# Quantizing the first feed-forward's input in parts of 704 and 320 columns, with all scale arithmetic on VectorE

## Chip, cores and metric

The program runs on one core of one Trainium2 chip, as one launch. The metric is device microseconds of that core, as the median of several executions. The kernel before has three: 3436.64, 3437.43 and 3438.43 us, with a median of 3437.43 us.

A core has five engines that work side by side, each on its own instructions in order: TensorE (PE: matmuls, with its weight loads listed apart as PEld), VectorE (DVE), ScalarE (ACT), GpSimd (POOL) and SyncE (SP, which here only issues transfers). They meet through semaphores. SBUF and PSUM are the on-chip memories, and PSUM holds what matmuls write; this stage uses eight PSUM tiles of one bank each (4, 3 and 1 in three pools).

## What is computed

The reference has two layers on an input of 8 sequences of 512 tokens with 256 channels. The change lies in the first layer:

```python
x = L0_attn_x                                   # (8, 512, 256)
xn = _layernorm(x)
x = x + _L0_attn_ref(xn, ...) + _L0_ffn_ref(xn, w_gate, w_up, w_down)
```

`_L0_attn_ref` is a selective state-space model. It projects `xn` to 512 channels, runs a causal convolution of four taps, and from the result makes a step size `delta`, and vectors `B` and `C` of 16 states. For each channel and state it runs the recurrence `h = exp(delta*A)*h + delta*u*B` over the 512 tokens, and sums `h*C` over the states.

`_L0_ffn_ref` is a gated feed-forward with 704 inner channels, and every operand of its three products is first rounded to four bits and back, block by block:

```python
def fp4_quant_dequant(x):                       # blocks of 16 along the last axis
    scale = max(max|block| / 6, 1e-12)
    q = round_to_grid(|block / scale|) * sign * scale
gate, y = fp4(xn) @ fp4(w_gate).T, fp4(xn) @ fp4(w_up).T
out = fp4(silu(gate) * y) @ fp4(w_down).T
```

The second layer is a block-sparse attention beside two layers of windowed attention with a gated feed-forward. The change does not touch it.

## The kernel before

**Two stages.** The first layer is one stage and the second layer another. In the first stage each engine gets its instructions in exactly the order in which the Python program issues them (class `Ordered`, L42). So the program order decides what stands behind what on each engine. The second stage starts when the first one's memory comes free, and is ordered by a planner.

**The main loop (L748).** A sequence ("batch" b, 8 of them) has 4 chunks of 128 channels, and a chunk has 16 states, taken two at a time. So a batch has 32 groups, and g counts 256 groups over the whole stage. Where a group's place in its batch matters, this text writes o = g - 32b. In each pass the loop issues, for its group: on ACT the decays of group g+1 (`da`), on PE the sum of an earlier group's states (`sum_states(g-2)`, tile `y`), on DVE the first scan of group g, on PE the spreading of B for group g+1 (`bu`), on POOL `times_c(g-1)` (tile `hh`, 128x1024), then one call of `step()`, on DVE the second scan of g, and on DVE `product(g+1)` (two instructions on tile `bu`). Because PE takes its instructions in order, `bu` of group g+1 stands behind `y` of group g-2, and that needs `times_c(g-2)` on POOL.

**Strands and steps.** All other work of the stage runs as generators, called strands here: `head(b)` makes norm, projection, convolution, step sizes and B and C of a batch; `ffn(b)` is the feed-forward; `output(b)` is the last projection; `z` is a gate branch; `fp4_weights` quantizes the weights. Each call of `step()` (L730) goes once through the active strands in the order in which they were started, and moves each by one step if PSUM allows:

```python
def step():
    for s, (peak, kept) in list(active.items()):
        if held[0] + peak <= MM:              # MM = 4 PSUM banks
            held[0] += kept
            active[s] = next(s, None)
```

A strand that needs more banks than are left stays where it is until a later step. `skewed(units, stages, every)` (L169) runs units through a list of stages, one stage to a step, and starts a unit every `every` steps; a tuple such as `(turn, 0, 1)` says how many banks a stage frees and takes. From L721 on, strands are started at fixed groups: `head(b+1)` at o = -5, `ffn(b)` at o = -1 (18 and 6 for b = 0 and 1), `output(b-1)` at o = 4.

**The gate at a batch's end.** Two groups before a batch begins, its first channel chunk must be ready, and if it is not, the loop calls further steps until it is, with no group's work between them:

```python
while g + 2 < total and at(g + 2)[:2] not in ready:
    step()
```

These are called extra steps below. A chunk is ready when `deltas(0)` of its head has been issued (L505). The head's stages between are `rank` (a matmul into one bank), `parts`, `second` (another bank), `third`, `fifth`, `logs`, `sums`, `deltas`; `third` and `fifth` each free a bank.

**The feed-forward strand (L524).** It first quantizes `xn` in place, then waits until the batch before has left its products (`busy`), transposes `xn` into `xqt` (two units, three steps), and then sends four tiles of 128 tokens, one every five steps, through 20 stages: five for gate and up products (in one bank), five to quantize the 128x704 result `h`, three to transpose it (`turn`, one bank), two for the down product (one bank), which `add` puts onto `x`. The text numbers the steps of this tile pipeline s0 to s29.

**Quantizing (L184).** `fp4_stages(p, f)` gives the stages for a tile of f columns, so n = f/16 blocks. Where n/4 is odd, one stage `inverses` does three things on DVE: the blocks' largest magnitude, the scale, and its reciprocal. Largest magnitudes and reciprocals lie there in rows of four used out of five places. Where n/4 is even, this is three stages: `scales` (DVE: largest magnitude), `scale` (POOL: scale, a 128x32 instruction) and `invert` (DVE: reciprocal). Then follow in both cases `divide` (POOL), `magnitude` (ACT), `levels` (DVE, two instructions) and `multiply` (POOL, two instructions). Before, `h` and `w_down` with 704 columns (n/4 = 11) go the first way; `xn` in two halves of 512 columns, and the gate and up weights, go the second (n/4 = 8).

Of the kernel before, what the change touches and what calls it, by code (L numbers as in the profile page):

```python
# [17 lines left out]
P = 128  # L18
NB, L, D = 8, 512, 256
NT = L // P  # L20
# [3 lines left out]
FI = 704  # L24
# [31 lines left out]
def tile_kernel(ctx: ExitStack, tc: tile.TileContext, a: dict, out: bass.AP):  # L56
# [57 lines left out]
    with ExitStack() as s0:  # L114
# [54 lines left out]
        def skewed(units, stages, every):  # L169


            made = {}
            stages = [s if isinstance(s, tuple) else (s, 0, 0) for s in stages]
            for step in range((len(units) - 1) * every + len(stages)):
                todo = [(i, stages[step - i * every]) for i in range(len(units)) if 0 <= step - i * every < len(stages)]
                peak = held = 0
                for _, (_, frees, takes) in todo:
                    held += takes - frees
                    peak = max(peak, held)
                yield peak, held  # L180
                for i, (f, _, _) in todo:
                    made[i] = f(units[i], made.get(i))

        def fp4_stages(p, f):  # L184

            n = f // QB

            def blocks(x):
                return x.rearrange("p (n b) -> p n b", b=QB)

            def spread(x):
                return x.unsqueeze(2).to_broadcast([p, n, QB])

            def inverses(_, x):


                amax = sm.tile([P, n // 4, 5], FP, tag="q_rows", name="q_rows")[:p, :, :4]
                sc = sm.tile([P, FI // QB], FP, tag="q_sc", bufs=4, name="q_sc")[:p, :n]
                r = sm.tile([P, n // 4, 5], FP, tag="q_ri", name="q_ri")[:p, :, :4]
                at = x.rearrange("p (a c b) -> p a c b", c=4, b=QB)  # L200
                dve.tensor_reduce(amax, at, AX.X, ALU.max, apply_absolute_value=True)
                dve.tensor_scalar(
                    sc.rearrange("p (a c) -> p a c", c=4), amax, 1.0 / 6.0, 1e-12, ALU.mult, ALU.max
                )
                dve.reciprocal(r, sc.rearrange("p (a c) -> p a c", c=4))
                return x, sc, r

            def scales(_, x):
                amax = sm.tile([P, FI // QB], FP, tag="q_amax", name="q_amax")[:p, :n]
                sc = sm.tile([P, FI // QB], FP, tag="q_sc", bufs=4, name="q_sc")[:p, :n]  # L210
                r = sm.tile([P, FI // QB], FP, tag="q_r", name="q_r")[:p, :n]
                dve.tensor_reduce(amax, blocks(x), AX.X, ALU.max, apply_absolute_value=True)
                return x, amax, sc, r

            def scale(_, st):
                x, amax, sc, r = st
                pool.tensor_scalar(sc, amax, 1.0 / 6.0, 1e-12, ALU.mult, ALU.max)
                return st

            def invert(_, st):  # L220
                x, amax, sc, r = st
                dve.reciprocal(r, sc)
                return x, sc, r

            def divide(_, st):
                x, sc, r = st
                v = q.tile([P, FI], FP, tag="q_v", bufs=3, name="q_v")[:p, :f]
                if len(r.shape) == 3:
                    quads = [y.rearrange("p (a c b) -> p a c b", c=4, b=QB) for y in (v, x)]
                    pool.tensor_tensor(*quads, r.unsqueeze(3).to_broadcast([p, *r.shape[1:], QB]), ALU.mult)  # L230
                else:
                    pool.tensor_tensor(blocks(v), blocks(x), spread(r), ALU.mult)
                return x, sc, v

            def magnitude(_, st):
                m = q.tile([P, FI], BF, tag="q_m", bufs=3, name="q_m")[:p, :f]
                act.activation(m, st[2], AF.Abs, scale=2.0**22)
                return *st, m

            def levels(_, st):  # L240

                x, sc, v, m = st
                dve.tensor_scalar(m, m, (1.0 + 2.0**-7) * 2.0**22, None, ALU.max)

                dve.scalar_tensor_tensor(v, v, 1.0 - 2.0**-23, m, ALU.mult, ALU.add)
                return st

            def multiply(_, st):
                x, sc, v, m = st
                pool.tensor_tensor(v, v, m, ALU.subtract)
                pool.tensor_tensor(blocks(x), blocks(v), spread(sc), ALU.mult)
                return x

            scaled = [inverses] if n // 4 % 2 else [scales, scale, invert]
            return [*scaled, divide, magnitude, levels, multiply]
# [265 lines left out]
        def ffn(b):  # L524

            x, xn = xs[b], made[b][0]

            def first(i, _):
                return xn[:, 2 * i : 2 * i + 2, :].rearrange("p t d -> p (t d)")

            scales, *stages = fp4_stages(P, 2 * D)
            yield from skewed(range(2), [lambda i, _: scales(i, first(i, _)), *stages], 3)
            yield 0, 0
            while b - 1 in busy:
                yield 0, 0
            busy.add(b)
            xqt = one.tile([P, KC, L], FP, tag="xqt", name="xqt")

            def turn_x(k, _):
                ps = pmm.tile([P, L], FP, tag="mm", name="ps_tr")  # L540
                for t in range(NT):
                    pe.transpose(ps[:, t * P : (t + 1) * P], xn[:, t, k * P : (k + 1) * P], ident)
                return ps

            def put_x(k, ps):
                act.copy(xqt[:, k, :], ps)

            yield from skewed(range(KC), [(turn_x, 0, 1), (put_x, 1, 0)], 1)
            n = FI // 2

            def product(t, w, cols):
                ps = pmm.tile([P, L], FP, tag="mm", name="ps_gu")
                for k in range(KC):
                    pe.matmul(
                        ps[:, :n], xqt[:, k, t * P : (t + 1) * P], w[:, k, cols],
                        start=(k == 0), stop=(k == KC - 1),
                    )
                return ps

            def gate_up(half):  # L560
                cols = slice(half * n, (half + 1) * n)

                def gate(t, h):
                    return h, product(t, w_g, cols)

                def up(t, st):
                    h, ps = st
                    act.activation(h[:, cols], ps[:, :n], AF.Silu)
                    if half and t == NT - 1:
                        busy.remove(b)  # L570
                    return h, product(t, w_u, cols)

                def both(t, st):
                    h, ps = st
                    dve.tensor_tensor(h[:, cols], h[:, cols], ps[:, :n], ALU.mult)
                    return h

                return gate, up, both

            def down(t, ht):  # L580
                ps = pmm.tile([P, L], FP, tag="mm", name="ps_d")
                for c in range(NI):
                    m = min(P, FI - c * P)
                    pe.matmul(
                        ps[:, :D], ht[:m, c, :], w_d[:m, c, :], start=(c == 0), stop=(c == NI - 1)
                    )
                return ps

            def add(t, ps):
                dve.tensor_tensor(x[:, t, :], x[:, t, :], ps[:, :D], ALU.add)  # L590

            def begin(t, _):
                return gate0(t, q.tile([P, FI], FP, tag="q_src", bufs=4, name="h"))

            (gate0, up0, both0), (gate1, up1, both1) = gate_up(0), gate_up(1)
            stages = [
                (begin, 0, 1), (up0, 1, 1), (lambda t, st: gate1(t, both0(t, st)), 1, 1), (up1, 1, 1), (both1, 1, 0),
                *fp4_stages(P, FI),
                *to_inner(lambda t: q.tile([P, NI, P], FP, tag="ht", name="ht")), (down, 0, 1), (add, 1, 0),
            ]  # L600
            yield from skewed(range(NT), stages, 5)
            done(b)
# [3 lines left out]
        def done(b):  # L606

            left[b] = left.get(b, 2) - 1
            if left[b] == 0:
                act.dma_start(x1_d[b], xs.pop(b))  # L610
# [840 lines left out]
```

## Time and profile before

One execution was also taken with the profiler.

| quantity | value |
|---|---|
| median of the runs | 3437.43 us |
| the profiled execution: its time / its span | 3434.61 us / 3432.7 us |
| first stage (start to the second stage's first matmul) | about 1409 us |
| last scan of the first stage ends | about 1378.9 us |
| busy over the span: PE, DVE, ACT, POOL | 91%, 70%, 51%, 46% |
| busy from 800 to 1000 us, of 200: PE, DVE, ACT, POOL | 176.9, 186.7, 147.7, 149.2 us |

The span goes from the first to the last instruction of the program; the execution's time is 1.9 us longer. In the list of groups, a line such as "DVE RECIPROCAL q_r<-q_sc 128x32 x16" names engine, operation, the written and the read tile, and how often it ran. In the first stage all instructions carry the line L50 of the recording helper, so they are told apart by tiles: `q_amax` and `q_rows` are the largest magnitudes (of the second and the first way), `q_sc` the scales, `q_r` and `q_ri` the reciprocals, `q_v` the divided values, `q_m` the magnitudes. A wait is put down to the instruction that released it.

### The profile page before, as it was taken

To read this page: it belongs to the slowest core of one execution; us is meant where nothing else is said; L and a number is where in the kernel's file an instruction comes from. 1 tells how busy PE (TensorE), PEld (TensorE's weight loads), DVE (VectorE), ACT (ScalarE), POOL (GpSimd) and SP (SyncE) were. 2 spreads that over 40 slices of the span, in tenths; PEclk is the share of its full clock that TensorE was granted. 3 is DMA by queue.
4 is the path that set the end of the run, shared out by engine and by line. 5 is a ranking of instruction groups with operands and counts; after the bars stand their busy time and mean duration, and the time that the engine had idled before them with its cause. 6 is when DMAs were issued, how large, how long until landed. Compare 5 with 4: busy or idle time off the path is not lost.

```text
span 3432.7 us, 41004 instructions
## 1 busy us (share of the span) xinstructions
PE 3125.9 (91%) x14082; PEld 1631.9 (48%) x14084; DVE 2420.1 (70%) x4792; ACT 1757.4 (51%) x3468; POOL 1584.3 (46%) x1141
## 2 busy tenths in 40 slices
PE   5768898889898988899999999999999999999998
PEld 2324454444444444455555455455445545545545
DVE  7979898989898999665466465566556456556544
ACT  5666777677776766244244244244334334433533
POOL 3786868787868687323133123123223223312312
PEclk7879999999999999899999999999999999999999
DMA  3323332323232323201101111111110100100100
GB/s 112 111 87 109 105 121 83 128 98 124 98 123 95 116 102 129 95 32 51 45 32 51 45 46 38 45 48 41 42 54 32 63 33 32 63 33 32 57 33 7
DMA packets 88856, 239.39 MB, mean 70 GB/s; under 512 B 9657, under 2 KB 42425, under 8 KB 88649
## 3 DMA queue, kind: packets, MB, share of 16 engines
q1 hardware_dynamic: 87496, 232.59, 19.6%
q10 hardware_dynamic: 1152, 4.19, 0.3%
q8 instruction: 112, 1.84, 0.2%
q14 instruction: 96, 0.78, 0.1%
HBM read 227.05 MB, written 9.70 MB: 69 GB/s over the span
## 4 chain that ended last, share of the span: by engine, by line
PE 59%; DVE 24%; POOL 7%; ACT 5%; issue 4%; DMA 1%; DVEq 0%; POOLq 0%; SPq 0%; ACTq 0%
PE ps_qkv L1105 10%; DVE hh L50 8%; PE ps_g L1284 5%; PE y L50 4%; PE ps_a L1284 4%; PE ps_wo L1248 3%; PE lo L1218 3%; DVE bu L50 3%; PE ps_y L1319 3%; PE ps_w L1302 3%; PE pt L1204 2%; POOL hh L50 2%; PE ps_ls L1157 2%; PE ps_gu L50 2%; DVE cv L50 2%
## 5 line engine op out<-in xcount | busy, mean ns | idle before, releaser
L50 POOL TENSOR_TENSOR hh<-hh,cb 128x1024 f32<-128x1024 f32 x256 | 604.0, 2361 | 297.7 <-DVE hh L50 129.6
L50 DVE TENSOR_TENSOR_SCAN hh<-da,bu 128x512 f32<-128x512 f32 x512 | 614.3, 1207 | 0.2 <-ACT da L50 0.2
L50 PE MATMUL y<-hh,ident 128*128 128x512 f32 x1024 | 520.1, 638 | 60.0 <-POOL hh L50 59.0
L50 ACT ACTIVATE da<-delta,a_neg 128x512 f32<-128x512 f32 x512 | 356.5, 718 | 326.1 <-DVE hh L50 317.5
L50 DVE TENSOR_TENSOR bu<-du,bu 128x512 f32<-128x512 f32 x512 | 325.5, 681 | 53.0 <-PE bu L50 51.9
L50 PEld LDWEIGHTS y<-hh,ident 128*128 128x128 f32 x1024 | 202.2, 204 | 291.9 <-issue 176.7
L50 ACT ACT_TABLE_LOAD x242 | 310.5, 1283 | 22.9 <-DVE x L50 9.6
L1195 POOL TENSOR_TENSOR pr<-pr,lrs 128x512 f32<-128x512 f32 (+1 forms) x256 | 234.7, 933 | 177.6 <-DVE lrs L1193 141.7
L1124 POOL TENSOR_TENSOR r<-r,r 128x512 f32<-128x512 f32 x128 | 162.9, 1272 | 288.9 <-DVE r L1122 243.5
L50 PE MATMUL bu<-bp,sel 128*128 128x512 bf16 x510 | 174.0, 393 | 125.3 <-DVE hh L50 124.4
L1176 ACT ACTIVATE pr<-ps_ls,nm 128x256 f32<-128x256 f32 (+1 forms) x512 | 221.5, 448 | 123.3 <-DVE nm L1170 120.2
L1120 DVE TENSOR_TENSOR r<-ps_qkv,tab 128x512 f32<-128x512 f32 x128 | 88.2, 689 | 201.6 <-ACT sq L1119 199.6
L1290 ACT ACTIVATE gl<-ps_g,b 128x512 f32<-128x512 f32 x96 | 65.9, 686 | 313.8 <-PE ps_g L1284 313.8
L1034 ACT ACTIVATE pt_e<-ps_st 128x512 f32<-128x512 f32 x320 | 166.6, 597 | 108.3 <-PE ps_st L1028 102.2
L873 POOL MEMSET sa<- 128x1 f32 x16 | 1.6, 98 | 449.9 <-DVE sf L1306 357.0
L1072 POOL TENSOR_TENSOR x1s<-x1s,bsum 128x256 f32<-128x256 f32 x32 | 23.1, 723 | 371.2 <-DVE x1s L1071 371.2
L1284 PE MATMUL ps_g<-hn,wf 128*128 128x512 f32 x384 | 189.6, 614 | 4.1 <-DVE hn L1273 2.6
L1291 DVE SCALAR_TENSOR_TENSOR ht<-ps_a,b,gl 128x512 f32<-128x512 f32 x80 | 60.1, 751 | 187.2 <-PE ps_a L1284 165.7
L1170 DVE CUSTOM_DVE_ANT_0 ps_ls<-ps_ls,mask 128x256 f32<-128x256 f32 (+1 forms) x512 | 184.3, 422 | 5.8 <-PE ps_ls L1157 4.9
L1105 PE MATMUL ps_qkv<-wqkv,sf 128*128 128x512 f32 x384 | 182.4, 607 | 0.0
L1105 PE MATMUL ps_qkv<-wqkv,s 128*128 128x512 f32 x384 | 181.4, 608 | 0.2 <-DVE r L1122 0.2
L1204 PE MATMUL pt<-ident,pr 128*128 128x128 f32 x896 | 132.1, 283 | 32.6 <-POOL pr L1195 28.1
(213 smaller groups left out, 6200.3 us busy)
## 6 DMA issues: line engine op xcount, KB each, us to landing
cb<-c_d SPq DMA_DIRECT2D x256, 512.0 KB, 3.6
wqkv<-in_wqkv SPq DMA_DIRECT2D x16, 1536.0 KB, 7.6
wf<-in_wf SPq DMA_DIRECT2D x16, 1408.0 KB, 11.4
wf<-in_wf SPq DMA_DIRECT2D x16, 768.0 KB, 4.3
tab<-tab SPq DMA_DIRECT2D x18, 512.0 KB, 3.5
wo<-in_wo SPq DMA_DIRECT2D x16, 512.0 KB, 3.9
x<-in_x SPq DMA_DIRECT2D x8, 512.0 KB, 4.9
x<-x ACTq DMA_DIRECT2D x8, 512.0 KB, 3.0
```

Of the source, the lines that this page charges most:

```text
L50: return self.tc.keep_in_program_order(getattr(self.engine, name)(*args, **kwargs))
L1034: act.activation(pt, banks[g], AF.Exp)
L1105: pe.matmul(ps, shifted(s, k, t * P, P), wqkv[:, k, i * IN : (i + 1) * IN], start=(k == 0), stop=(k == KC - 1),)
L1124: pool.tensor_tensor(r1[:, i], r1[:, i], r2, ALU.add)
L1170: last = dve.tensor_tensor_reduce(at, at, msk[:, 2 * P - nk :], -1.0, 3e38, ALU.add, ALU.min, nm[:, i : i + 1])
L1176: act.activation(pr[:, at], banks[r][:, at], AF.Exp, bias=nm[:, i : i + 1], scale=-1.0, accum_out=rs[:, i : i + 1],)
L1195: pool.tensor_tensor(ph, ph, rs.unsqueeze(2).to_broadcast([P, 2, nk]), ALU.mult)
L1204: pe.transpose(pt[:, j * P : (j + 1) * P], pr[:, j * P : (j + 1) * P], ident)
L1218: pe.matmul(o[r * LD : (r + 1) * LD, i * P : (i + 1) * P], lv[:, keys[j], h * LD : (h + 1) * LD], prts[r][:, (i * nkt + j) * P : (i * nkt ...
L1248: pe.matmul(ps, wo[:, c, m * P : (m + 1) * P], ot[:, c, :], start=(c == 0), stop=(c == IN // P - 1),)
L1284: pe.matmul(dst, wf1[:, k, off : off + P], hn[:, k, :], start=(k == 0), stop=(k == KC - 1))
L1302: pe.matmul(ps, wf2[:n, c, m * P : (m + 1) * P], ht[c][:n], start=(c == 0), stop=(c == NHC - 1),)
```

## The change

`xn`, which lies as 1024 columns in each partition (4 token tiles of 256 channels), is quantized as one part of 704 columns and one of 320, in place of two halves of 512. The numbers of blocks are 44 and 20, n/4 is 11 and 5, both odd. So both parts go the way of `inverses`: the largest magnitude, the scale and the reciprocal all come from DVE in one stage, in the rows of four of five, and the stages `scale` on POOL and `invert` on DVE fall away for `xn`. The list of stages shrinks from seven to five; the second part still starts three steps after the first. All blocks of 16 and their arithmetic stay the same. The weights keep their stages.

```diff
             x, xn = xs[b], made[b][0]
-            def first(i, _):
-                return xn[:, 2 * i : 2 * i + 2, :].rearrange("p t d -> p (t d)")
-
-            scales, *stages = fp4_stages(P, 2 * D)
-            yield from skewed(range(2), [lambda i, _: scales(i, first(i, _)), *stages], 3)
+            flat = xn.rearrange("p t d -> p (t d)")
+            parts = [(flat[:, :FI], fp4_stages(P, FI)), (flat[:, FI:], fp4_stages(P, NT * D - FI))]
+            stages = [lambda i, st, k=k: parts[i][1][k](i, st if k else parts[i][0]) for k in range(len(parts[0][1]))]
+            yield from skewed(range(2), stages, 3)
             yield 0, 0
             while b - 1 in busy:
```

## The prediction

> **What bounds the kernel now.** I read the page's busy shares by slice first: the first stage (the left 16 of 40 slices) is bound by VectorE, with GpSimd close behind.
>
> ```profile
> DVE  7979898989898999665466465566556456556544
> ...
> POOL 3786868787868687323133123123223223312312
> ```
>
> Then the tile view of the scales:
>
> ```profile
> L50 DVE TENSOR_SCALAR q_sc<-q_rows x34: 198/199/200, 196.8 to 1388.5; 128x44 f32<-128x44 f32 x34
> L50 DVE RECIPROCAL q_ri<-q_sc x34: 428/429/430, 197.1 to 1388.7; 128x44 f32<-128x44 f32 x34
> ...
> L50 POOL TENSOR_SCALAR q_sc<-q_amax x24: 314/333/649, 66.2 to 1263.0; 128x32 f32<-128x32 f32 x16, 88x32 f32<-88x32 f32 x8
> L50 DVE RECIPROCAL q_r<-q_sc x24: 317/345/353, 70.9 to 1264.1; 128x32 f32<-128x32 f32 x16, 88x32 f32<-88x32 f32 x8
> ...
>   POOL q_sc L50: 8.1, 3
> ```
>
> Three times, 8.1 us in all, VectorE stood still for a 0.33 us scale. The timelines of POOL and DVE around one of these (b = 5) say why:
>
> ```profile
> 918.91 2.36 POOL L50 TENSOR_TENSOR hh<-hh,cb 128x1024 f32<-128x1024 f32 x1
> 921.25 2.42 POOL L50 TENSOR_SCALAR xn<-x,ln_mv,ln_rs 128x256 f32<-128x256 f32 x2
> 923.74 0.33 POOL L50 TENSOR_SCALAR q_sc<-q_amax 128x32 f32<-128x32 f32 x1
> ```
>
> ```profile
> 920.05 0.52 DVE L50 TENSOR_TENSOR h<-h,ps_gu 128x352 f32<-128x352 f32 x1 [0.26 <-PE ps_gu L50]
> 924.10 0.35 DVE L50 RECIPROCAL q_r<-q_sc 128x32 f32<-128x32 f32 x1 [3.53 <-POOL q_sc L50]
> ```
>
> POOL was late by a whole queue: it ran without a gap from 889.55 to 952. The wait is a symptom of that queue. Last, DVE's busy time by stretch (columns: stretch, length, busy), o = -4 to 12 around the starts of batches 2 and 5:
>
> ```profile
> 384.30:480.60 96.30, 84.13 (x119) 0.93 0.27 93
> ...
> 885.80:974.50 88.70, 79.79 (x111) 0.92 0.28 95
> ```
>
> Batch 2's start idles 12.2 us, batch 5's 8.9 (3 and 6: 14.1 and 8.2; 4: 7.5). Before batches 2 and 3 the loop made extra steps, before 4 to 7 none.
>
> **What the skill says.** "VectorE: DVE Perf Modes", What auto-detection actually checks: a single-source op takes a two-port mode if its outermost sizes are even or equal; the rows of four of five with 11 or 5 quads are meant against that. "SBUF — State Buffer", Who interferes with whom: VectorE in a two-port mode, or with two SBUF inputs, and GpSimd block each other for a whole instruction. The trace agrees: `q_m` in place takes 277 to 2360 ns, while the 128x44 `q_sc` never leaves 198 to 200.
>
> **The instructions.** Before, a batch costs DVE 2 x (0.647 largest magnitude + 0.349 reciprocal) = 1.99 us (groups of 740 to 1240 us). After, the 704 part costs 0.865 + 0.199 + 0.428 = 1.49 (rows of `h`). No row has the 320 form: lines through the two measured widths give 0.43 + 0.27, and the 20-wide scale lies between 0 and 0.199; I take 0.17, so 0.87 (ends 0.68, its share by width, and 1.0). DVE: +0.37 a batch, +3.0 in eight (ends +1.4 and +4). POOL loses 2 x 0.327 = 0.65 a batch; its divides and multiplies, ACT's magnitudes and `levels` keep their columns, and lines through their 512 and 704 rows keep their sums. No transfer is added. New wait: `levels` of part 0 comes at step 3 behind ACT's magnitude and POOL's divide at step 1. Behind it on DVE stand the second scan and `product`; POOL's queue below puts divide's end before that point, so I charge nothing; uncovered it costs up to the old 3.5 us in four batches.
>
> **The moved order.** Quantizing takes 3 + 5 = 8 steps, before 3 + 7 = 10. So `ffn`'s tile pipeline starts two steps earlier, at o = 12 for 14, and meets `head` at another point for the four banks. I counted banks by hand. The count for before reproduces the trace: batch 4's third tile is one step late (its first half product of `h` in group 155, not 154), as `head` holds 3 banks at o = 24 and the pipeline's s10 needs 2.
>
> After, s10 falls on o = 22. `head` takes 2 there and holds 3; s10 waits to o = 23, and pipeline and `head` hold 2 each. `head`'s second `second` needs a bank at o = 24 and gets it at 26. Everything of the head is two steps late; `deltas(0)`, which came at o = 29, exactly when the gate at o = 30 wants it, comes too late: two extra steps before each of batches 4 to 7. Earlier batches by the same count: 5 extra steps before batch 1 become 6 (`z` holds a bank when `second` wants two), 2 before batch 2 become 0, 4 before batch 3 become 2.
>
> **Price of batches 4 to 7.** In extra steps POOL gets sums and deltas (1.27 us each, `deltas` two of them) without group work between. POOL's queue from `times_c(28)` to the end of `times_c(31)`: before 9.0 (o = 29: `times_c` 2.36, two deltas, one sum, one tile's `multiply` 2.9) + 6.2 (30) + 6.3 (31) + 2.4 (`times_c(31)`) = 23.8 (trace: 889.55 to 913.3); after, 3.6 (o = 29), 15.0 (30: three sums, two deltas, a divide, two norms, `times_c`), 10.2 (31) and 2.4 = 31.2. `product` of the group after o = 1 needs that and some 2.3 us of `y` and `bu`: with 1.4 of lag 34.9. DVE is there at 30.5: five groups at 3.4 (the shortest in the trace), 10.7 of strands by their rows (a tile's first stage 1.46 twice and the 704 part's 1.49, `levels` 2.7, norms' statistics 2.1, two halves of `h` 0.9, two small ones), and 2.4 waiting in the extra steps for ACT, where two Silus and a Ln follow each other with a 1.28 table load each. So DVE waits 2.4, some 4.2 here and 0.9 later: 7.5. Before, batch 5 had 1.4, 3.8 (the `q_sc` wait in it) and 2.1 = 7.3. The gain of the removed wait is spent: 0 net (POOL's 0.65 against the 0.2), bounds -1.5 and +4 each. +4 is what batch 2 showed with two extra steps (12.2 against 8.2).
>
> **Early batches and tail.** Batch 2 without extra steps: POOL's same sum, with the feed-forward's tiles six groups later, is 19.6, which DVE's own work outlasts: no wait for POOL, -5 (ends -2 and -7.6, the stretch's whole difference). Batch 3: idle 14.1 falls to some 8.5 to 12.2: -5 (ends -2, -6). Batch 1: one more latency-bound step: +1.5 (ends 0, +4; its five steps took 21.5 us for a group). Tail: the last tile is two steps earlier against the last scan. But in PE's order its transposes then stand ahead of all four of `output(7)`'s `ps_o` steps, which wait with them for POOL: by the rows the stage ends at 1402 in place of 1403.5, -1.5 (ends +2, -6). The second stage starts by the first one's end; its order I leave.
>
> **The sum.** +3.0 + 0 - 5 - 5 + 1.5 - 1.5 = -7.0 us. The profiled run took 3434.6 (span 3432.7 and 1.9 around it), so 3427.6 for such a run. The median of the runs is 2.8 higher; I put the difference on it: 3430 us.
>
> **Rivals.** (B) Slower: POOL's queue at the late batches becomes the bound. Price p per start is +4, as batch 2 showed; batch 2 gains 4 and batch 3 2: +3.0 + 16 - 4 - 2 + 1.5 - 1.5 = +13, 3450. For it: POOL is gapless there already; against: part of batch 2's idle came with a later feed-forward. It decides from p = 2.8 (-7 + 5p = +6.9, batch 3 counted). (C) p between 0 and 2.8: the pieces cancel, about 3437. (D) The count of banks is wrong, extra steps stay: at most -8.1 + 3.0 - 1.5 = -6.6 if the waits go whole, 3431; for it: only the 8.1 is measured; against: the count fits the trace. (E) The rows of 20 fall into a two-port mode, the change doesn't do what it says, and scales wait for POOL again: up to 8 x 2.4 = +19, 3456; against: 44 never did.
>
> **Chances.** A (forecast) 0.38, own range 3423 to 3431; D 0.10, half of it faster; C 0.20; B 0.28; E 0.02; 0.02 elsewhere slower. 0.2% is 6.9 us, about what a measurement tells from no change. Faster 0.43; same 0.25 (C and half of D); slower 0.32. The range holds A's bounds and B: 3418 to 3452.
>
> **What would show it.** Right: no `q_r` for `xn`, 16 `q_sc` of 20 and 44 columns more on DVE; the reciprocals' 8.1 us wait gone; from batch 4 on, norms (`xn`, POOL) before a batch's first scan and a DVE wait for `bu` near o = 1; batch 2's start idle below 9. Wrong: no such wait, or one above 8 us; a quantized part's `levels` waiting long for ACT; the last scan earlier with the end unmoved.

## The result, and the profile after

The changed kernel takes 3455.31 us (median of four runs, 3451.53 to 3461.02) against 3437.03 us before it (3436.51 to 3438.43): a ratio of 1.0052, interval 1.0039 to 1.0066. It is slower by 18 us. The prediction was 3430 us with a range up to 3452, so sign and range were both missed. The profiled execution took 3451.53 us with a span of 3449.3 us, 16.6 us more than the span before.

The busy shares by slice of the kernel after show the same two engines close to full in the first stage:

```profile
DVE  7989898989898999665566466466456556556544
...
POOL 3786768686868686333133133123123222312412
```

VectorE (DVE) is busy for 2449.7 us instead of 2420.1, although the new instructions account for 3.2 us of that. The tile view of the scales of the kernel after (shortest, median and longest duration in ns):

```profile
L50 DVE TENSOR_SCALAR q_sc<-q_rows x50: 174/199/200, 149.8 to 1398.2; 128x44 f32<-128x44 f32 x42, 128x20 f32<-128x20 f32 x8
L50 DVE RECIPROCAL q_ri<-q_sc x50: 277/428/432, 150.0 to 1398.4; 128x44 f32<-128x44 f32 x42, 128x20 f32<-128x20 f32 x8
...
L50 POOL TENSOR_SCALAR q_sc<-q_amax x8: 314/516/654, 65.5 to 142.9; 88x32 f32<-88x32 f32 x8
```

The sixteen 128x32 scales have left GpSimd (POOL), and the wait of 8.1 us for them is gone. The change does what it says. Now DVE's busy time around the starts of batches 2 and 5 (o = -4 to 12; columns: stretch, length, busy):

```profile
388.90:482.80 93.90, 88.28 (x117) 0.93 0.25 90
...
891.60:986.20 94.60, 82.70 (x112) 0.95 0.30 100
```

Batch 2's start is 2.4 us shorter than before (93.90 against 96.30). It idles 6.6 us less, but 4.15 us of that came back as longer busy time. Batch 5's start is 5.9 us longer (94.60 against 88.70): 3.0 us of idle and 2.9 us of busy time. Batches 4, 6 and 7 show +6.2, +5.7 and +5.1. These four starts make 22.9 us together; that is where the time went.

POOL's timeline at batch 5's start, from `times_c(28)` (at 896.04) to `times_c(0)` (at 930.23):

```profile
896.04 2.36 POOL L50 TENSOR_TENSOR hh<-hh,cb 128x1024 f32<-128x1024 f32 x1
...
905.96 2.36 POOL L50 TENSOR_TENSOR hh<-hh,cb 128x1024 f32<-128x1024 f32 x1
...
912.74 2.42 POOL L50 TENSOR_SCALAR xn<-x,ln_mv,ln_rs 128x256 f32<-128x256 f32 x2
915.13 2.35 POOL L50 TENSOR_TENSOR hh<-hh,cb 128x1024 f32<-128x1024 f32 x1
...
925.36 2.34 POOL L50 TENSOR_TENSOR hh<-hh,cb 128x1024 f32<-128x1024 f32 x1
...
930.23 2.35 POOL L50 TENSOR_TENSOR hh<-hh,cb 128x1024 f32<-128x1024 f32 x1
935.23 4.67 POOL L50 TENSOR_TENSOR hh<-hh,cb 128x1024 f32<-128x1024 f32 x2
939.86 1.37 POOL L50 TENSOR_TENSOR u<-u,z 128x512 f32<-128x512 f32 x1
```

Between one `hh` and the next lie 7.6, 6.8 and 7.9 us of other POOL work, with no gap from 890.78 to 941. From the start of `times_c(28)` to the end of `times_c(31)` (the `hh` at 925.36) are 31.7 us. In the kernel before, the first and the last of these four are

```profile
889.55 2.36 POOL L50 TENSOR_TENSOR hh<-hh,cb 128x1024 f32<-128x1024 f32 x1 [2.71 <-DVE hh L50]
...
910.95 2.36 POOL L50 TENSOR_TENSOR hh<-hh,cb 128x1024 f32<-128x1024 f32 x1
```

so it was 23.8 us there. DVE's timeline of the changed kernel in the same place:

```profile
923.16 2.32 DVE L50 TENSOR_TENSOR_SCAN hh<-da,bu 128x512 f32<-128x512 f32 x2
932.00 1.29 DVE L50 TENSOR_TENSOR bu<-du,bu 128x512 f32<-128x512 f32 x2 [6.52 <-PE bu L50]
...
938.41 1.69 DVE L50 TENSOR_SCALAR q_m<-q_m 128x704 bf16<-128x704 bf16 x1
940.21 1.77 DVE L50 SCALAR_TENSOR_TENSOR q_v<-q_v,q_m 128x704 f32<-128x704 f32 x1
941.90 0.33 DVE L50 TENSOR_SCALAR q_m<-q_m 128x704 bf16<-128x704 bf16 x1
942.34 0.89 DVE L50 SCALAR_TENSOR_TENSOR q_v<-q_v,q_m 128x704 f32<-128x704 f32 x1
```

Two losses stand side by side here. DVE waits 6.52 us for the spread B of the next group, which stands on PE behind the sum that needs `times_c`. Right after that, `levels` (two instructions, `q_m<-q_m` and `q_v<-q_v,q_m`) runs twice with the same shape. The first pair takes 1.69 + 1.77 us, the second, with POOL idle from 941.2 to 945.4, 0.33 + 0.89. This agrees with what the Trainium skill says in "SBUF — State Buffer", Who interferes with whom: a DVE instruction in a two-port mode or with two SBUF inputs waits until a running GpSimd instruction is through. POOL was in the two `hh` until 939.90 and in `u` until 941.23.

Over the whole stage, what the `levels` instructions take above such undisturbed durations (the short ones of each width; called the `levels` excess below) grew from 48.8 to 70.2 us, and DVE's idle time between first and last scan fell from 110.9 to 98.4 us. The extra steps before batches 1 to 7 were 5, 2, 4, 0, 0, 0, 0 and are 6, 0, 2, 2, 2, 2, 2.

### The profile page after: what moved, and what is told of

The parts are those of the page before. It is cut to its first block, busy times and chain, and to the rows that moved or that the text cites. A ratio compares the mean times of both kernels' runs of the same rounds, so it can differ in the third digit from the quotient of the medians.

```text
span 3449.3 us, 41019 instructions
## 1 busy us (share of the span) xinstructions
PE 3123.7 (91%) x14084; PEld 1629.3 (47%) x14084; DVE 2449.7 (71%) x4808; ACT 1779.5 (52%) x3485; POOL 1575.9 (46%) x1125
## 3 DMA queue, kind: packets, MB, share of 16 engines
q1 hardware_dynamic: 87496, 232.59, 19.6%
## 4 chain that ended last, share of the span: by engine, by line
PE 50%; DVE 8%; ACT 2%; POOL 1%; issue 1%; DMA 0%; DVEq 0%; POOLq 0%; ACTq 0%
PE ps_qkv L1105 10%; PE ps_g L1284 5%; PE ps_a L1284 4%; PE ps_wo L1248 3%; PE lo L1218 3%; PE ps_y L1319 3%; PE ps_w L1302 3%; PE pt L1204 2%; PE ps_ls L1157 2%; DVE nm L984 2%; PE pt_qk L1096 1%; PE ps_st L1030 1%; PE ps_qk L926 1%; PE o L1012 1%; PE ps_st L1028 1%; DVE ps_ls L1170 1%
## 5 line engine op out<-in xcount | busy, mean ns | idle before, releaser
L50 PE MATMUL y<-hh,ident 128*128 128x512 f32 x1024 | 529.7, 648 | 54.7 <-POOL hh L50 53.5
```

Of the source, the lines that this page charges most:

```text
L50: return self.tc.keep_in_program_order(getattr(self.engine, name)(*args, **kwargs))
```

## The experiments

Two explanations were open after this. Either the longer `levels` instructions (+21.4 us, more than the whole loss) are the cause, a fight for SBUF that comes with the new quantizing itself. Or the cause is the place: two stages fewer move the feed-forward's tiles, that makes the head late, and the extra steps stack POOL's queue. The first four kernels ran against 3438.79 us for the kernel before (32 runs), the other four against 3437.59 us (16 runs). A profiled first stage of the same kernel repeats to about 2 to 4 us, as the last two kernels show.

**E1: the new instructions in the old places.** Two idle stages behind the first give the second way the old ten steps.

```diff
             stages = [lambda i, st, k=k: parts[i][1][k](i, st if k else parts[i][0]) for k in range(len(parts[0][1]))]
+            stages[1:1] = [lambda i, st: st] * 2
             yield from skewed(range(2), stages, 3)
```

> Two theories. Place: the loss comes from where the feed-forward's steps now fall (VectorE's two `levels` instructions waiting for GpSimd's port, extra steps before batches 4 to 7). Instructions: it comes from the scale and the wider forms put on VectorE. This kernel keeps the changed instructions and puts two idle stages behind the first, so that every later step falls where it fell before. Place expects 3430 to 3441 us, extra steps 5, 2, 4, 0 as before, `levels` some 49 us above their undisturbed durations as before (70 in the changed kernel), and the reciprocal's 8.1 us gone or partly returned as other waits. Instructions expects 3448 to 3458.

Measured: 3428.15 us, ratio 0.9975 (0.9966 to 0.9984), 2 us under the range named for place. The extra steps are those of before, the `levels` excess is 48.5 us, and DVE no longer waits for a `q_sc`. So the instructions by themselves cost nothing that shows in the total; the loss of 18 us belongs to the order. The gain of 0.25% is a separate matter, taken up with E7 and E8.

**E2: the idle steps behind the quantizing.** Here the quantizing keeps its short form and only the tiles go back to their old place.

```diff
             yield from skewed(range(2), stages, 3)
+            yield 0, 0
+            yield 0, 0
             yield 0, 0
             while b - 1 in busy:
```

> The changed kernel with two idle steps behind the five stages: quantizing falls where the change put it, the tiles where they were. If the tiles' earlier place (and with it the extra steps) is the cause, 3430 to 3442 us and extra steps 5, 2, 4, 0. If the earlier place of the quantizing itself is, 3446 to 3458 with `levels` still some 65 to 70 us above undisturbed. Instructions expects 3448 to 3458.

Measured: 3438.49 us, ratio 1.0004 (0.9996 to 1.0012). Extra steps are as before the change, and batch 5's start takes 89.9 us. The `levels` excess is 61.1 us, 12 more than before, and DVE's idle time 97.1 us, 14 less. So `xn`'s `levels`, two steps earlier, do run into POOL's queue, yet this costs nothing that shows in the total: what the instructions stretch is, by these two numbers, no longer waited for elsewhere. (In the one profile of E2 the first stage is 4.8 us longer than in that of the kernel before, 1414.1 against 1409.25, and the second 3.8 us shorter.) That leaves the shift of the tile pipeline.

**E3: the old instructions with an early feed-forward.** The kernel before, with each `ffn` started two groups sooner.

```diff
-            start(g + 18 if b == 0 else g + 6 if b == 1 else g - 1, (ffn, b))
+            start(g + 16 if b == 0 else g + 4 if b == 1 else g - 3, (ffn, b))
```

> The kernel before, with the feed-forward strand started two groups earlier and its instructions untouched: the tiles fall where the change puts them. Place expects 3445 to 3460 us, with two extra steps before each of batches 4 to 7 (the head's third and fifth stages four groups apart). Instructions expects 3433 to 3441.

Measured: 3474.4 us, ratio 1.0108 (1.0094 to 1.0122): slower by 36 us without any of the new instructions, and 14 us above the range named for place. The extra steps are those of the changed kernel, two before each of batches 4 to 7. DVE's busy time in batch 5's start, and what DVE waited for in it:

```profile
905.10:1002.80 97.70, 82.19 (x106) 0.86 0.29 96
```

```profile
DVE bu L50 <- PE bu L50: 10.3, 6, 5.4
```

The same wait as after the change, here of 5.4 us at the longest, and a stretch of 97.70 us. The edit also moves the quantizing: POOL's queue from `times_c(28)` to the end of `times_c(31)` now holds a scale and a divide of `xn` too and is 34.9 us. So the size of the loss cannot be carried over; that an early tile pipeline brings the extra steps and the wait for `bu` is shown.

**E4: the changed kernel, its third tile held back.** A tile has 15 stages (5 + 5 + 3 + 2), not the 20 given above, and starts five steps after the one before it. So at s10 the first tile begins its transposes and the third its first gate product, one bank each. Three idle steps ahead of s10 bring it to o = 25, behind the point where `head` needs the banks. Quantizing and the first ten steps stay early.

```diff
-            yield from skewed(range(NT), stages, 5)
+            for i, need in enumerate(skewed(range(NT), stages, 5)):
+                if i == 10:
+                    yield 0, 0
+                    yield 0, 0
+                    yield 0, 0
+                yield need
             done(b)
```

> The changed kernel with the tile pipeline held for three steps before its eleventh, so that it asks for its two banks after the head has freed its own: quantizing and the first two tiles as in the changed kernel, no extra steps before batches 4 to 7. If the extra steps carry the loss, 3432 to 3442 us. If the earlier quantizing and first tiles carry it by port waits alone, 3446 to 3456 with `levels` 65 us or more above undisturbed.

Measured: 3431.12 us, ratio 0.9974 (0.9964 to 0.9983), 24 us less than the changed kernel and 1 us under the range named for the extra steps. The extra steps before batches 1 to 7 are 6, 1, 1, 0, 0, 0, 0. Batch 5's start on DVE, and all waits that the profile lists for it there:

```profile
885.20:975.10 89.90, 86.30 (x113) 0.96 0.28 93
```

```profile
DVE x L50 <- PE ps_o L50: 0.9, 1, 0.9
DVE h L50 <- PE ps_gu L50: 0.7, 2, 0.4
DVE q_v L50 <- DVE q_m L50: 0.5, 1, 0.5
DVE q_m L50 <- ACT q_m L50: 0.4, 1, 0.4
```

The wait for `bu` is gone, and the stretch takes 89.90 us instead of 94.60. The `levels` excess over the stage is 69.4 us, the same as in the changed kernel (70.2), while DVE's idle time falls to 82.3 us. Equal port waits with the whole loss undone: longer `levels` are not what costs the 18 us.

The hold moves the tiles' later stages together with the extra steps, so E4 alone does not say which of the two counts. POOL's queue before batch 5 does. Its first and last `hh` in E4, again `times_c(28)` and `times_c(31)`:

```profile
889.01 2.35 POOL L50 TENSOR_TENSOR hh<-hh,cb 128x1024 f32<-128x1024 f32 x1 [3.31 <-DVE hh L50]
...
910.45 2.35 POOL L50 TENSOR_TENSOR hh<-hh,cb 128x1024 f32<-128x1024 f32 x1
```

That is 23.8 us, as in the kernel before and in E1 and E2, against 31.7 in the changed kernel. In all of them the queue holds four `hh` (9.4 us) and the same three feed-forward instructions (one tile's `multiply` and another's `divide`, 4.3 us). The 7.9 us that the changed kernel has more are work of heads that the two extra steps bring forward: the next head's `sums` and `deltas` take 14.6 us in place of 11.5, with two `sums` more, and the norms of the head after it take 4.9 us. Batches 4 and 6 show the same. Batch 2, which loses its two extra steps by the change, shows the reverse: its queue falls from 32.1 to 21.4 us and the idle time of its start from 12.2 to 5.6. The queue's length is not the whole price, though: before batch 7 there is no further head, its queue has no norms and grows by 3.1 us only, and its start is still 5.1 us longer. A kernel that has the extra steps and nothing else moved was not run.

**E5 and E6: after and before without `levels` in SBUF.** In both kernels the two `levels` instructions become two reductions into a small tile. In both traces no reduction takes more than 35 ns above the shortest of its form (the first ones of 128 partitions 319 to 354 ns), so they do not wait for POOL. Both kernels leave the rounding to four bits out.

```diff
-                act.activation(m, st[2], AF.Abs, scale=2.0**22)
+                act.activation(m, st[2], AF.Abs, scale=2.0**-22)
 ...
-                dve.tensor_scalar(m, m, (1.0 + 2.0**-7) * 2.0**22, None, ALU.max)
-                dve.scalar_tensor_tensor(v, v, 1.0 - 2.0**-23, m, ALU.mult, ALU.add)
+                few = sm.tile([P, n // 4, 5], FP, tag="q_rows", name="q_few")[:p, :, :4]
+                at = [y.rearrange("p (a c b) -> p a c b", c=4, b=QB) for y in (m, v)]
+                dve.tensor_reduce(few[:, :3], at[0][:, :3], AX.X, ALU.max)
+                dve.tensor_reduce(few, at[1], AX.X, ALU.max)
```

> The changed kernel with the two instructions of `levels` replaced by two reductions that write a small tile, so that nothing on VectorE there reads two SBUF tensors[...]; the rounding to four bits is left out (ScalarE scales the magnitudes down so that the values stay finite), all other instructions and their order stay. Against its twin from the kernel before: if the port waits of `levels` carry the loss, the difference between the twins falls from 18 us to below 6. If POOL's queue and the extra steps carry it and the port only shows it, the difference stays at 12 us or more, and the waits appear as idle time before `product` or before the reductions.

> The kernel before with the same replacement of `levels` (the rounding to four bits left out), as the twin of the one above. Alone it should be faster than the kernel before by some of the 49 us that `levels` loses there, 10 to 40 us.

Measured: 3428.29 us (ratio 0.9972, 0.9964 to 0.9981) for the changed kernel and 3411.42 us (0.9929, 0.9912 to 0.9945) for the one before. The changed kernel is still 16.9 us slower, inside the 12 us or more named for POOL's queue and the extra steps; the twin gains 26 us, inside its 10 to 40. Batch 5's start on DVE and the two longest waits in it, first of the changed kernel without `levels` (E5):

```profile
877.50:969.20 91.70, 76.76 (x113) 0.94 0.30 103
```

```profile
DVE bu L50 <- PE bu L50: 9.6, 4, 7.5
DVE x L50 <- PE ps_o L50: 2.3, 2, 1.5
```

then the stretch of the kernel before without them (E6):

```profile
868.90:956.70 87.80, 76.47 (x111) 0.96 0.27 95
```

With busy times alike (76.76 and 76.47 us), the stretch is 3.9 us longer in E5, 3.6 us of it idle, and its longest wait for `bu` is 7.5 us. POOL's queue is 31.1 us in E5 and 23.8 in E6. Over the starts of batches 4 to 7 the difference is 16.6 us (3.4, 3.9, 3.4, 5.9), of 22.9 us with `levels` in place. So the contention carries up to about a quarter of the loss there, and the place of the work the rest. The total of the first stage does not fall with it (1406.1 against 1383.1 us, 23.0 apart, where 1428.8 and 1409.25 are 19.6 apart): batch 0, 2.8 us shorter after the change, is 5.0 us longer in E5 than in E6; why is open. The profiled run of E6 is also the fastest of its four, 6.9 us under their median.

**E7 and E8: before and E1 again, one run each.** No edit; they were to say in which stage E1's gain lies.

> The kernel before, unchanged, profiled on the chip of this call beside the next kernel: a first stage within 5 us of 1409 us and a second within 8 us of 2023, both following the granted clock.

> The changed instructions in the old places once more, to see in which stage its 0.25% lies. If the removed wait for the scale gives it, the first stage is 4 to 9 us shorter than that of the kernel before beside it; if only the granted clock of the second stage does, the first stages agree within 3 us or this one is longer.

Measured: 3436.03 and 3425.97 us. The first stage lasts 1411.3 us and 1409.0 us (in the first profiles 1409.25 for before, 1413.25 for E1). The means are 1410.3 for the kernel before and 1411.1 for E1's, so E1 gains nothing there. The second stage lasts 2022.8 us in E7 (2023.5 in the first profile of before), and 2015.1 us in E8 (2015.2 in E1). All of E1's gain lies in a stage that the change does not touch. PE's busy time and granted clock (the fourth number) there, first of the kernel before, then of E1:

```profile
2000.00:2350.00 350.00, 339.51 (x1824) 0.99 0.11 40
2350.00:2700.00 350.00, 337.78 (x1833) 0.99 0.12 43
```

```profile
2000.00:2350.00 350.00, 338.80 (x1853) 1.00 0.12 41
2350.00:2700.00 350.00, 336.78 (x1821) 1.00 0.12 42
```

The clock is a little higher in E1. In that stage each engine's instructions stand in the same order in both kernels. Averaged over the whole second stage, the granted clock of the traces is 0.986 and 0.985 in the two profiles of the kernel before, and 0.991 and 0.992 in the two of E1's. The single profiles of the other six kernels lie between these ends, with 0.986 to 0.988 and 2019.5 to 2023.1 us. So a shorter second stage goes with a higher clock. No run sets the clock, so that it is the cause of the 8 us is not shown, and what raises it stays open.

## Why the prediction failed

Its terms, and what the two traces show for them (the starts are the stretches from o = -4 to 12, less 0.4 us each for the new instructions):

| term | predicted | measured |
|---|---|---|
| DVE's instructions | +3.0 | +3.2 |
| start of batch 1 | +1.5 | +2.2 |
| start of batch 2 | -5 | -2.8 |
| start of batch 3 | -5 | -1.6 |
| starts of batches 4 to 7 | 0 | +21.3 |
| rest of the scans | 0 | -3.9 |
| tail (last scan to second stage) | -1.5 | +1.1 |
| second stage | 0 | -3.0 |
| sum | -7.0 | +16.5 |

**Right.** The prices: a 320-column part's largest magnitude, scale and reciprocal take 0.477, 0.174 and 0.278 us, a 704-column part's 0.837, 0.199 and 0.428, in all 2.39 us a batch against some 2.0 before. The rows of 20 stay out of the faster mode (rival E falls: 0.174 us in all eight). The count of banks by hand gave each batch's extra steps exactly (rival D falls). Norms stand before a batch's first scan, with a wait for `bu` near o = 1, as forecast. POOL's queue was worked out as 31.2 us and is 31.7. Batch 2's start idles 5.6 us, under the 9 that was named; its queue was worked out as 19.6 us and is 21.4.

**Wrong: the price of batches 4 to 7.** It set DVE's waits at 7.5 us after against 7.3 before and called the gain of the removed wait spent, 0 net. Measured for batch 5 is 11.9 against 8.9 us of idle, and 2.9 us more of busy time, 0.4 of it the new instructions. Three terms of the sum were mis-sized. The wait for `bu` was to be 4.2 us (34.9 less 30.5 is 4.4, and the pieces named for the 30.5 add up to 30.1) and is 6.5: DVE is there 29.4 us after the start of `times_c(28)` and not 30.5, and `product` runs 36.0 us after it and not 34.9. The later waits are 2.1 us (for the products of the last projection, `ps_o`, and of the feed-forward, `ps_d`) instead of 0.9. And the busy time was counted as columns only: "its divides and multiplies, ACT's magnitudes and `levels` keep their columns, ... keep their sums". They keep their columns, but at the new place `levels` stand against a POOL queue with no gaps, and their excess in batch 5's start is 6.4 us in place of 3.9. These three are 2.3, 1.2 and 2.5 us, 6.0 together, where the start lost 5.5 beside the new instructions. The bounds of -1.5 and +4 a start were too narrow as well: measured is +5.3.

The longer `levels` alone did not decide, though it looks so in the trace. E2 and E4 have 12 and 21 us more of `levels` excess than before and are not slower in total, and E5 against E6 keeps most of the loss without it. A wait for the port and a wait for a late POOL result are two ways to meet the same queue; counting one without the other, as the prediction did with idle time, gives a wrong sum. The starts of batches 2 and 3, forecast at -5 each and measured at -2.8 and -1.6, missed for the third of these reasons: batch 2's idle time fell by 6.6 us, more than the forecast, and batch 3's to 11.3 us, inside it, but DVE's busy time rose by 4.15 and 1.6 us.

**The rival that came.** B named the mechanism, POOL's queue at the late batches, with p = +4 a start; it decides from 2.8. Measured is p = 5.3 (21.3 / 4). E4 shows that the price goes when the two extra steps and the early place of the later tiles go, and the make-up of POOL's queue there puts its growth down to the extra steps. It got 0.28 because the trace before showed POOL already without gaps and the removed waits seemed to pay for the rest; the evidence for +4, batch 2's 12.2 us of idle with its two extra steps against 8.2 in batch 6 without any, was in the same views and served only as a bound and for B.

**The tail.** Forecast as -1.5 with ends of +2 and -6, measured +1.1; no experiment was made on it. The second stage was put at nothing and came out 3.0 us shorter, in the direction of its clock (0.988 against 0.986).

## What to carry to other kernels

When an edit shortens a list of pipeline steps, everything behind it moves; count first where the shared slots (here four PSUM banks) are then short, and pin the old place with idle steps where the new one is worse (E1, E4: 3428 and 3431 us, without the loss; that they also lie under the kernel before is not shown to come from the idle steps, as E1's gain lies in the second stage and E4's first stage is only 2.4 us shorter, no more than it repeats to). Price a pile-up on one engine by the length of its queue up to the result that others need. Take port waits and idle time of the waiting engine as one sum, since removing one may only turn it into the other.

## What was not expected of the hardware

- Longer instructions without a longer stage: E4 has 69.4 us of `levels` excess, 20.6 us more than the kernel before, and its first stage takes 1406.9 us against 1409.25.
- A second stage with the same order of instructions took 2015.1 and 2015.2 us in two profiles of E1's kernel and 2022.8 and 2023.5 us in two of the kernel before, with a mean granted clock of 0.992, 0.991, 0.985 and 0.986 in it.
